# Cross-attention with nested Winograd products: column sums of a softmax taken from inner right sums, and one right sum made by ScalarE and a transfer

## Chip, cores and metric

The kernel runs on one core of a Trainium2 chip. The metric is the device time of one execution in microseconds (us). All data is float32.

## What is computed

Eight independent batches, each with x1 and x2 of 512 channels by 1024 positions. Constants: a projection to 64 channels for queries and keys, and a 512 by 512 matrix for the values.

```python
B, C1, C2, N = (8, 512, 512, 1024)
q = jnp.einsum('bcn,dc->bnd', x1, Wq) + bq
k = jnp.einsum('bcn,dc->bdn', x2, Wk) + bk[:, None]
v = jnp.einsum('bcn,dc->bdn', x2, Wv) + bv[:, None]
attn = jax.nn.softmax(jnp.einsum('bnd,bdm->bnm', q, k), axis=2)
attn_out = jnp.einsum('bcm,bnm->bcn', v, attn)
return attn_out + x1
```

## The kernel before

**Order of the two large products.** The kernel applies the value matrix last: with e the exponentials of the scores, it forms y = x2 · e, divides y by the column sums of e, and multiplies by Wv (`w`). So each batch has two matrix products: y (512 x 1024 times 1024 x 1024) and the output (512 x 512 times 512 x 1024). The scores lie transposed, with the keys m on partitions: in tile `e` of half h (512 queries n each), `e[:, g, i, :]` holds 128 keys by 512 queries, two groups g of four tiles i.

**Products of products.** Each of the two is split in 2 x 2 blocks and computed with Winograd's seven products instead of eight (table `MULT`): the left factors are 11, 12, 22 and the sums S1 to S4 of blocks of the left matrix (`LEFT`), the right ones 11, 21, 22 and the sums T1 to T4 of blocks of the right matrix. They come in the order 1, 2, 6, 7, 5, 3, 4. Many of the seven are split once more in the same way (the inner products). For such an inner product, number i, `left_stream` makes its four left sums on VectorE in four pieces of 256 columns (L522, tile `aI`), and `right_stream` its right sums in three pieces: T1 and T3 together (L537, 1024 columns), T2 (L542, 512), T4 (L544, 512). The tiles are called after the product: eI1 is product 1, eI2 product 2, eI6 product 6, eI7 product 7. Products 1 and 2 of y take right blocks of the exponentials of half 0 themselves, tiles g = 0 and g = 1; products 6, 7, 5 and 4 take outer sums, product 3 the exponentials of half 1. Product 6 is split for batches 2 to 5 only. On TensorE an inner product is a run of matmuls at L555 into the banks `chain` and `third`; ScalarE's copies (L746) carry partial results from `chain` to the banks of the outer product (`ps_ya`, `ps_yc`).

**One period.** `period(s, n, nn, nnn)` does the rest of batch s and the beginning of batch n, the next one: all its products but the first few are for s, and the scores, the softmax and the first sums for n are put between. Every engine's queue is written out by hand: the order of calls in `period` is the order in which each engine runs its instructions, and `weave` takes one operation in turn from several streams. Nothing is reordered at run time; an instruction that waits holds up all that follow on its engine.

**Softmax of half 0 of batch n**, during batch s: the maximum (`highest`), subtraction of it (`lower`, VectorE L322), exponentials in place (`exponential`, ScalarE L331). The column sums are then made as follows:

- `copy_first`: ScalarE copies the first tile of e into `sum` (L971, 1024 columns).
- `add_tile`, three times: a transfer that GpSimd issues adds another tile of e to `sum` (L966, 512 KB each).
- `total`: VectorE adds the two groups (`fold_halves`, L266, 512 columns), GpSimd sums over the partitions (L291, `den`), and a transfer spreads row 0 of it over 128 partitions x 4 columns (`few`).
- `invert`: VectorE's reciprocal of `few` (L299), and a transfer to a row in DRAM; `spread`: a transfer that brings that row to all partitions. `scale_y` (L875) multiplies blocks of y by it.

**End of a period** (L1505 on), where one batch hands over to the next. The output of batch s ends with product 4 (`second(4)`, TensorE L464 into the banks `ps_oc`, with T4 of y as its right factor, tile `yT`), while VectorE makes the sums of products 1 and 2 of batch n. Then come `total(n, 0)` and `evict_o(s, "21")`: VectorE adds to block 21 of the output what two banks `ps_oc` hold (L937, tile `o`, two instructions of 512). In the next period TensorE starts with products 1 and 2 of y; the copies of product 2's chain (L746, `ps_yc`) write into the banks that this eviction empties. Then VectorE makes S2 of product 6 and the others (L522).

**T4 of y** (a right sum of the outer output product) is `sum_y(s, "T4")`, a VectorE subtraction of 1024 columns: y21 − T2 (L429). In batches 1 to 6 it stands in the handover behind the first left sums of product 1 of batch n, ahead of the first right sums (L537, eI1) and the addition to `ps_oc` (L719), which ends output product 7. Before that addition ScalarE copies a part to the same bank (L711).

Of the kernel before, what the change touches and what calls it, by code (L numbers as in the profile page):

```python
# [9 lines left out]
F32 = mybir.dt.float32  # L10
AF = mybir.ActivationFunctionType
ALU = mybir.AluOpType
# [3 lines left out]
def kernel(  # L16
# [47 lines left out]
    nc = tc.nc  # L64
    P = 128
    B, C, N = x1.shape
    D = 64
    CT = C // P
    H = 512
# [5 lines left out]
    sb = ctx.enter_context(tc.tile_pool(name="sb", bufs=1))  # L75
# [188 lines left out]
    def fold_halves(s, h, op):  # L264
        f = s.mx[h]
        nc.vector.tensor_tensor(f[:, 0, :], f[:, 0, :], f[:, 1, :], op)  # L266
# [29 lines left out]

    def invert(s, h):

        nc.vector.reciprocal(s.few[h], s.few[h])  # L299
        s.row[h] = row = dram.tile([1, H], F32, tag="row", name=f"row_{s.b}_{h}")  # L300
        nc.gpsimd.dma_start(row.rearrange("o (p f) -> (o p) f", p=P), s.few[h])

    def spread(s, h):

# [117 lines left out]
    def sum_y(s, k):  # L422
        y = s.y
        if k == "T2":
            for n in ("T1", "T2", "T4"):
                y[n] = sb.tile([P, 2, H], F32, tag=f"y{n}", name=f"y{n}_{s.b}")
            nc.vector.tensor_tensor(y["T2"], y["11"], y["T3"], ALU.add)
        else:
            nc.vector.tensor_tensor(y[k], y["22" if k == "T1" else "21"], y["T2"], ALU.subtract)  # L429

    HALVES = left, right = slice(0, H // 2), slice(H // 2, H)


# [45 lines left out]
    def multiply_o1(s):  # L479
# [34 lines left out]

    def left_stream(s, i, x, tag):

        v = {f"{p + 1}{q + 1}": x[:, ts(q, MH // 2), ts(p, P)] for p in range(2) for q in range(2)}
        sums = sb.tile([P, 4, MH // 2, P], F32, tag=tag, name=f"aI{i}_{s.b}")
        s.inner[i] = v
        for z, (k, x, y, op) in enumerate(LEFT):  # L520
            v[k] = sums[:, z]
            nc.vector.tensor_tensor(v[k], v[x], v[y], op)  # L522
            yield
# [4 lines left out]
    def right_stream(s, i, x, *tags):  # L528

        half = x.shape[1] // 2  # L530
        v = {f"{q + 1}{r + 1}": x[:, ts(q, half), ts(r, H // 2)] for q in range(2) for r in range(2)}
        last = 4 // len(tags)
        shape = [P, last, half, H // 2]
        sums = [sb.tile(shape, F32, tag=t, name=f"eI{i}{t}_{s.b}") for t in tags]
        both, t2, t4 = sums[0][:, 0:2], sums[-1][:, last - 2], sums[-1][:, last - 1]
        part = x.rearrange("p (q k) (r n) -> p q k r n", q=2, r=2)
        nc.vector.tensor_tensor(  # L537
            both, part[:, :, :, 1, :], part[:, 0].rearrange("p k r n -> p r k n"), ALU.subtract
        )
        s.inner[i, "t"] = v | {"T1": both[:, 0], "T3": both[:, 1], "T2": t2, "T4": t4}  # L540
        yield
        nc.vector.tensor_tensor(t2, both[:, 0], v["22"], ALU.subtract)  # L542
        yield
        nc.vector.tensor_tensor(t4, v["21"], t2, ALU.add)  # L544
        yield
# [326 lines left out]
    def scale_y(s, *ks):  # L872
        for k in ks:
            rden = s.rden[k in ("T3", "22")].unsqueeze(1).to_broadcast([P, 2, H])
            nc.vector.tensor_tensor(s.y[k], s.y[k], rden, ALU.mult)  # L875
# [120 lines left out]
    def head_keys(s, n, bank):  # L996
# [3 lines left out]
        def add(*tiles):  # L1000
            for c in tiles:
                for h, r in ((0, lo), (1, hi)):
                    nc.tensor.matmul(
                        ps[r, n], wk_sb[:, c, :], s.x[:, c, HALVES.index(n), h], start=(c == 0), stop=(c == CT - 1)
                    )
# [5 lines left out]
    def head(s):  # L1011
# [101 lines left out]
    def period(s, n, nn, nnn):  # L1113

        late = s.b >= 1
        five = late and n is not None
# [36 lines left out]
                highest(n, 0)  # L1153
            return then

        def add_exponential(i):
            exponential(n, 0, i)
            add_tile(n, 0, i)

        def while_11(j):  # L1160
            if five and j == 0 and nn:
                add_exponential(3)

        def while_57(j):
            if nn:
                exponential(n, 1, j)
            elif j == 0:
                add_exponential(3)
# [7 lines left out]
        def first_sum():  # L1176
            copy_first(n, 0)
            add_tile(n, 0, 1)

        if not s.t:  # L1180
            open_t(s)
# [178 lines left out]
        if n:  # L1360
            if s.b:
                load_a(n, "11")
            if nn is None:
                load_x(n, x1)
            if nn:
                scores_and(n, 1, 2, "a", nothing)
            else:
                scores(n, 1, 0)()
                scores(n, 1, 1)()
                third = scores(n, 1, 2, "a")  # L1370
                third(0)
# [34 lines left out]
        if five:  # L1406
            fold(n, 1, 3, "max", ALU.max)
            products = multiply_41(s)
            next(products)
            highest(n, 1)  # L1410
            next(products, None)
            if s.six:
                exponential(n, 0, 2)
            if nn is None:
                first_sum()
                begin_s1(n)
                end_s1(n)
        elif late:
            weave(multiply_41(s))
        else:  # L1420
            multiply_seeded(s, 4, "r", hooks)()
            begin_s1(n)
            end_s1(n)
# [52 lines left out]
        if n:  # L1476
            if five:
                sums_1 = left_stream(n, 1, n.a["11"], "i2")
                next(sums_1)
                weave(sums_1, singly(lambda: lower(n, 1, 2), lambda: sum_y(s, "T4")))  # L1480
        if n is None:
            inner_right(s, "o3", s.y["22"], "eT2")
            multiply_573(s)
# [35 lines left out]
        if n:  # L1519
            weave(  # L1520
                in_turn(
                    sums_n1 if s.six else right_stream(n, 1, n.e[0][:, 0], "yT1", "yT2"),
                    singly(*([lambda: lower(n, 1, 3)] if s.b == 0 else [])),
                    right_stream(n, 2, n.e[0][:, 1], "eT4"),
                ),
                left_stream(n, 2, n.a["12"], "aI3" if n.b > 1 else "aS4"),
            )
            last = evict_o(s, "12")
            if five:
                negate(n, "S3")  # L1530
# [50 lines left out]
```

## Time and profile before

| | |
|---|---|
| runs, us | 664.44, 665.40, 666.31 (median 665.4) |
| profiled execution: span from first to last instruction | 662.5 us |
| granted clock of TensorE | 1.000 |
| TensorE matmuls (PE) | 657.7 us busy, 99% of the span |
| VectorE (DVE) | 622.4 us, 94% |
| ScalarE (ACT) | 379.7 us, 57% |
| GpSimd (POOL) | 225.5 us, 34% |
| DMA queue q0 (software_dynamic) | 50.4% of 16 DMA engines' span |
| DMA queue q1 (hardware_dynamic) | 30.6% |

The page gives the span of the profiled execution and no other time of it; the runs in the first row are executions of their own, and the difference of their median and the span is 2.9 us.

How to read rows. A row of the groups reads: line, engine, operation, out<-in by the program's names (batch numbers left out), partitions x elements, how many times; behind the bar busy time, mean duration of one in ns, and idle time ahead of it with what ended most of it. In a timeline a row begins with the start in us from the span's start and the duration in us of one instruction or a run of equal ones (x2, x4); in square brackets may stand how long the engine was idle ahead of it and what it waited for. In the waits of an engine stand: engine, line waiting, what was waited for, us in total, times, longest. In a table of windows stand the window, its length, busy time of TensorE and number of its matmuls, then weight loads, VectorE, ScalarE, GpSimd, and at the end granted clock, share of the DMA engines and GB/s; the first two numbers behind the window are its length and TensorE's busy time. On PE a line of the kernel shows its matmuls, on PEld the loads of their weights.

### The profile page before, as it was taken

What the parts mean: (1) busy time and instruction counts of PE and PEld (TensorE: products, weight loads), DVE (VectorE), ACT (ScalarE), POOL (GpSimd) and SP (SyncE); (2) the same over time, 40 slices, a digit from 0 to 9 for tenths busy, and PEclk for the clock granted to TensorE, in tenths of its full rate; (3) what the DMA queues carried; (4) which work ended last, traced back from release to release, by engine and by line L of the source; (5) the groups of instructions that cost most, each with busy time, mean ns of one, the idle gap of its engine ahead of it and who ended that gap; (6) DMA issues with size and microseconds to landing.
All of it is one profiled execution on the core that took longest, in us unless ns stands there. A gap on an engine that the chain in (4) does not pass through costs nothing.

```text
span 662.5 us, 7988 instructions
## 1 busy us (share of the span) xinstructions
PE 657.7 (99%) x2626; PEld 433.7 (65%) x2626; DVE 622.4 (94%) x869; ACT 379.7 (57%) x728; POOL 225.5 (34%) x192
## 2 busy tenths in 40 slices
PE   9999999999999999999999999999999999999997
PEld 4435755756658666677666686576865757666865
DVE  1999999999999998999989999899999989999997
ACT  3755557446475575665756647656576555574332
POOL 0125215631255412463126431364213640244300
PEclk9999999999999999999999999999999999999999
DMA  8688578994899859998599995998948994399604
GB/s 329 259 281 255 118 256 147 210 261 142 276 162 227 240 164 299 194 245 198 166 290 204 227 232 148 276 209 203 273 91 192 216 243 176 77 180 242 132 15 152
DMA packets 51545, 135.88 MB, mean 205 GB/s; under 512 B 5680, under 2 KB 6192, under 8 KB 51504
## 3 DMA queue, kind: packets, MB, share of 16 engines
q0 software_dynamic: 24512, 61.94, 50.4%
q1 hardware_dynamic: 26848, 73.29, 30.6%
q8 instruction: 21, 0.34, 0.2%
q10 hardware_dynamic: 144, 0.14, 0.1%
q14 instruction: 20, 0.16, 0.1%
HBM read 87.83 MB, written 16.81 MB: 158 GB/s over the span
## 4 chain that ended last, share of the span: by engine, by line
PE 98%; DMA 1%; SPq 0%; DVE 0%; issue 0%
PE ps_yc L555 9%; PE ps_ya L555 7%; PE ps_oc L464 7%; PE ps_oa L689 7%; PE ps_s L236 6%; PE ps_ya L464 4%; PE ps_oa L464 4%; PE ps_q L191 4%; PE ps_i5chain L555 3%; PE ps_i4b L840 3%; PE ps_k L191 3%; PE ps_i3chain L555 3%; PE ps_i7chain L555 3%; PE ps_oc L840 3%; PE ps_i1chain L555 3%; PE ps_i2chain L555 3%
## 5 line engine op out<-in xcount | busy, mean ns | idle before, releaser
L331 ACT ACTIVATE e<-e 128x1024 f32<-128x1024 f32 x60 | 63.4, 1059 | 25.6 <-DVE e L322 25.2
L291 POOL PARTITION_ALL_REDUCE den<-sum x16 | 52.8, 3298 | 59.0 <-DVE sum L266 54.2
L322 DVE TENSOR_TENSOR e<-e,top 128x1024 f32<-128x1024 f32 x60 | 72.3, 1217 | 0.2 <-POOL top L272 0.2
L272 POOL PARTITION_ALL_REDUCE top<-max x16 | 31.4, 1960 | 94.1 <-DVE max L266 68.1
L966 POOL DMA_DIRECT2D sum<-e x21 | 25.9, 1235 | 82.0 <-ACT sum L971 32.6
L245 ACT COPY e<-ps_s 128x512 f32<-128x512 f32 x90 | 47.8, 622 | 10.1 <-PE ps_s L236 7.6
L236 PE MATMUL ps_s<-q,k 64*128 64x512 f32 (+1 forms) x188 | 46.6, 598 | 0.0
L256 DVE TENSOR_TENSOR max<-max,e 128x1024 f32<-128x1024 f32 x30 | 36.6, 1218 | 0.3
L236 PEld LDWEIGHTS ps_s<-q,k 64*128 64x128 f32 x188 | 17.5, 186 | 19.9 <-issue 17.4
L875 DVE TENSOR_TENSOR y<-y,den 128x1024 f32<-128x1024 f32 x24 | 29.2, 1220 | 0.3
L522 DVE TENSOR_TENSOR aI<-a,aI 128x256 f32<-128x256 f32 x60 | 28.1, 468 | 0.9
L746 ACT COPY ps_yc<-ps_i7chain 128x256 f32<-128x256 f32 x32 | 11.4, 357 | 30.2 <-PE ps_i7chain L555 26.1
L689 PE MATMUL ps_oa<-yT,w_S 128*128 128x512 f32 x56 | 27.4, 592 | 0.0
L307 POOL DMA_DIRECT2D den<-row x12 | 6.7, 558 | 59.0 <-DMA row<-few 47.8
L522 DVE TENSOR_TENSOR aI<-a 128x256 f32<-128x256 f32 x60 | 26.3, 464 | 0.0
L689 PE MATMUL ps_oa<-y,w_S 128*128 128x512 f32 x56 | 26.3, 592 | 0.0
L191 PE MATMUL ps_q<-x_in_x_dram,wqk_sb 128*64 128x512 f32 x112 | 25.6, 598 | 0.0
L746 ACT COPY ps_ya<-ps_i5chain 128x256 f32<-128x256 f32 x32 | 11.5, 361 | 24.2 <-PE ps_i5chain L555 20.0
L464 PE MATMUL ps_oa<-yT,w_S 128*128 128x512 f32 x56 | 25.2, 593 | 0.0
L464 PE MATMUL ps_oc<-yT,w 128*128 128x512 f32 x56 | 25.2, 592 | 0.0
L555 PE MATMUL ps_yc<-e,aI 128*128 128x256 f32 x92 | 23.6, 379 | 0.0
L746 ACT COPY ps_ya<-ps_i1chain 128x256 f32<-128x256 f32 x28 | 10.0, 357 | 22.1 <-PE ps_i1chain L555 18.5
(346 smaller groups left out, 1840.0 us busy)
## 6 DMA issues: line engine op xcount, KB each, us to landing
x_in_x_dram<-in_x_dram SPq DMA_DIRECT2D x60, 512.0 KB, 7.9
a<-in_x2T_dram SPq DMA_DIRECT2D x32, 512.0 KB, 7.0
aS<-in_x2T_dram POOLq DMA_DIRECT2D x21, 512.0 KB, 10.2
sum<-e POOLq DMA_DIRECT2D x21, 512.0 KB, 6.2
eT<-eT POOLq DMA_DIRECT2D x16, 512.0 KB, 11.9
r<-in_x_dram POOLq DMA_DIRECT2D x14, 512.0 KB, 8.3
uo<-in_x_dram POOLq DMA_DIRECT2D x14, 512.0 KB, 9.8
out_dram<-r SPq DMA_DIRECT2D x14, 512.0 KB, 8.9
```

Of the source, the lines that this page charges most:

```text
L191: nc.tensor.matmul(ps[r, :], w_sb[:, c, :], s.x[:, c, ts(h, H)], start=(c == 0), stop=(c == CT - 1),)
L236: nc.tensor.matmul(ps[g][:, n], s.k[r, ts(i, P)], s.q[r, ts(h, H)][:, n], start=True, stop=True)
L245: nc.scalar.copy(e[:, g, i, :], ps[g])
L256: nc.vector.tensor_tensor(f, e[:, :, 0, :] if i == 1 else f, e[:, :, i, :], op)
L291: nc.gpsimd.partition_all_reduce(s.den[h], s.mx[h][:, 0, :], P, ReduceOp.add)
L322: nc.vector.tensor_tensor(e, e, top, ALU.subtract)
L331: nc.scalar.activation(e, e, AF.Exp)
L464: nc.tensor.matmul(ps, left[ka][:, k, ts(j, P)], right[kb][:, k, :], start=opens and k == 0, stop=i in (2, 3, 4) and k == n_k - 1, skip_gr ...
L522: nc.vector.tensor_tensor(v[k], v[x], v[y], op)
L555: nc.tensor.matmul(ps, s.inner[i][ka][:, k, :], s.inner[i, "t"][kb][:, k, :], start=opens and k == 0, stop=z in (2, 3, 4) and k == n_k - 1 ...
L689: nc.tensor.matmul(ps, w[ka][:, k, ts(j, P)], s.y[kb][:, k, :], start=False, stop=i == 3 and k == 1, skip_group_check=True,)
L840: nc.tensor.matmul(ps, s.inner[i][ka][:, k, :], s.inner[i, "t"][kb][:, k, :], start=opens and k == 0, stop=z in (2, 3, 4) and k == n_k - 1 ...
```

## The change

**Column sums of half 0** for batches 2 to 7 (`total_0`). For inner products 1 and 2, whose right blocks are tiles of e, the inner sums get other signs: the left ones by the table `LEFT_SUM`, and the right ones are T1 = 12 − 11, T3 = 22 + 12, T2 = T1 + 22, T4 = 21 − T2. The products stay equal. With these signs T4 + T3 is 21 + 11 and T3 is 22 + 12: the sums over the two row blocks of that part of e. They are made by four VectorE pieces of 512 columns (L573) instead of three pieces. Left pieces keep their number and size. `total_0` adds the T4/T3 pairs of products 1 and 2 in one VectorE instruction of 1024 columns (L282), whose output order interleaves the two halves of columns in runs of 4; the fold of halves, the sum over partitions and a transfer follow as before, the last to 64 partitions x 8 (`fews`). `invert` adds the two halves of that small tile (64x4, L316) ahead of the reciprocal (64x8). For batches 2 to 7 the copy of the first tile and the three transfers are gone; the exponentials stay where they were. Batch 1 keeps the old way.

**T4 of y** for batches 1 to 5. `copy_yt4`: ScalarE writes −T2 (1024 columns, L450) right behind the last copies of the products 4 and 1 (`multiply_41`). A transfer from GpSimd adds block 21 of y to it (L1463), once that has been scaled. The subtraction on VectorE is gone there; batches 0, 6 and 7 keep it.

```diff
+    def total_0(s):
+        s.mx[0] = f = sb.tile([P, 2, H], F32, tag="fold", name=f"sum_{s.b}_0", bufs=2)
+        x, y = (s.inner[i, "m"].rearrange("q z k (p f) -> q z k p f", p=D) for i in (1, 2))
+        nc.vector.tensor_tensor(f.rearrange("q k (p z f) -> q z k p f", p=D, z=2), x, y, ALU.add)
+        fold_halves(s, 0, ALU.add)
+        s.den[0] = sb.tile([P, H], F32, tag="den", name=f"den_{s.b}_0", bufs=2)
+        nc.gpsimd.partition_all_reduce(s.den[0], f[:, 0, :], P, ReduceOp.add)
+        s.few[0] = sb.tile([D, 2, H // P], F32, tag="fews", name=f"fews_{s.b}", bufs=2)
+        nc.gpsimd.dma_start(
+            s.few[0].rearrange("p z f -> p (z f)"), s.den[0][0:1, :].rearrange("o (p f) -> o p f", p=D)
+        )
...
     def invert(s, h):
-        nc.vector.reciprocal(s.few[h], s.few[h])
+        few = s.few[h]
...
+        if h == 0 and s.b > 1:
+            nc.vector.tensor_tensor(few[:, 0, :], few[:, 0, :], few[:, 1, :], ALU.add)
+            to = row.rearrange("o (z p f) -> (o p) z f", z=2, p=D)
+        nc.vector.reciprocal(few, few)
+        nc.gpsimd.dma_start(to, few)
...
+    def copy_yt4(s):
+        nc.scalar.mul(s.y["T4"], s.y["T2"], -1.0)
...
+    LEFT_SUM = (
+        ("S3", "21", "11", ALU.subtract),
+        ("S1", "21", "22", ALU.subtract),
+        ("S2", "11", "S1", ALU.subtract),
+        ("S4", "12", "S2", ALU.subtract),
+    )
...
+            for k, x, y, op in (
+                ("T1", "12", "11", ALU.subtract),
+                ("T3", "22", "12", ALU.add),
+                ("T2", "T1", "22", ALU.add),
+                ("T4", "21", "T2", ALU.subtract),
+            ):
+                nc.vector.tensor_tensor(v[k], v[x], v[y], op)
+                yield
...
-            elif nn:
-                first_sum()
...
+            if nn:
+                copy_yt4(s)
             if s.six:
                 exponential(n, 0, 2)
             if nn is None:
-                first_sum()
                 begin_s1(n)
                 end_s1(n)
...
         scale_y(s, "21")
+        if five and nn:
+            nc.gpsimd.dma_start(s.y["T4"], s.y["21"], accum_op=ALU.add)
...
-        if s.six:
-            add_tile(n, 0, 2)
-        elif five:
-            add_exponential(2)
+        if five and not s.six:
+            exponential(n, 0, 2)
...
             second(4)
-            total(n, 0)
+            if five:
+                total_0(n)
+            else:
+                total(n, 0)
             evict_o(s, "21")
```

**Where it moves instructions.** VectorE's queue in the handover from batch 2 to batch 3, from behind the sum of outer blocks to the eviction of block 21 of the output. Each row has the line, the operation, the tile written, the tiles read and the shape (names end in the batch and a running number); eI1 and eI2 are right sums of products 1 and 2, aI left sums of product 2, `e_0` the exponentials of half 0. Before:

```order
L542 TENSOR_TENSOR eI1yT_3_1814<-eI1yT_3_1813,e_0_1446 128x512
L522 TENSOR_TENSOR aI_3_1830<-a_3_1734 128x256
L544 TENSOR_TENSOR eI1yT_3_1814<-e_0_1446,eI1yT_3_1814 128x512
L522 TENSOR_TENSOR aI_3_1830<-a_3_1734 128x256
L537 TENSOR_TENSOR eI2eT_3_1834<-e_0_1446 128x1024
L522 TENSOR_TENSOR aI_3_1830<-a_3_1734,aI_3_1830 128x256
L542 TENSOR_TENSOR eI2eT_3_1834<-eI2eT_3_1834,e_0_1446 128x512
L522 TENSOR_TENSOR aI_3_1830<-a_3_1734,aI_3_1830 128x256
L544 TENSOR_TENSOR eI2eT_3_1834<-e_0_1446,eI2eT_3_1834 128x512
L266 TENSOR_TENSOR sum_0_1649<-sum_0_1649 128x512
L937 SCALAR_TENSOR_TENSOR o_2_1854<-ps_oc_2_7_1779,wqk_sb,uo_2_1754 128x512
```

And now (lines of the changed kernel; L550 is the old L522, L978 the old L937):

```order
L573 TENSOR_TENSOR eI1yT_3_1813<-e_0_1449 128x512
L550 TENSOR_TENSOR aI_3_1829<-a_3_1735 128x256
L573 TENSOR_TENSOR eI1yT_3_1812<-eI1yT_3_1812,e_0_1449 128x512
L550 TENSOR_TENSOR aI_3_1829<-a_3_1735 128x256
L573 TENSOR_TENSOR eI1yT_3_1813<-e_0_1449,eI1yT_3_1812 128x512
L550 TENSOR_TENSOR aI_3_1829<-a_3_1735,aI_3_1829 128x256
L573 TENSOR_TENSOR eI2eT_3_1835<-e_0_1449 128x512
L550 TENSOR_TENSOR aI_3_1829<-a_3_1735,aI_3_1829 128x256
L573 TENSOR_TENSOR eI2eT_3_1835<-eI2eT_3_1835,e_0_1449 128x512
L573 TENSOR_TENSOR eI2eT_3_1835<-e_0_1449,eI2eT_3_1835 128x512
L282 TENSOR_TENSOR sum_0_1850<-eI1yT_3_1813,eI2eT_3_1835 128x2x128x4
L266 TENSOR_TENSOR sum_0_1850<-sum_0_1850 128x512
```

Ten rows stood ahead of the eviction (L937), and thirteen stand there now: a row of eI2 that reads the same as its neighbour (the second piece of product 2, behind the fourth aI) is left out above, and the eviction follows behind the last row. Of product 1's pieces T1 alone is made further up; before, T1 and T3 were. The new sum of 1024 columns (L282) stands between the last right sum and the fold, in the place of nothing, and reads that right sum.

GpSimd's queue in the same period (batch 2, the softmax of batch 3), from the sums of exponentials to the loads for the output. Before:

```order
L966 DMA sum_0_1649<-e_0_1446 128x2x512
L169 DMA aS_3_1652<-in_x2T_dram 128x1024
L272 ISA top_1_1725<-max_1_1676 128x512
L966 DMA sum_0_1649<-e_0_1446 128x2x512
L900 DMA uo_2_1754<-in_x_dram 128x2x512
L966 DMA sum_0_1649<-e_0_1446 128x2x512
L942 DMA r_2_1765<-in_x_dram 128x2x512
L181 DMA aS_3_1810<-in_x2T_dram 128x1024
```

And now (L941 is the old L900, L983 the old L942):

```order
L169 DMA aS_3_1652<-in_x2T_dram 128x1024
L272 ISA top_1_1725<-max_1_1676 128x512
L1463 DMA yT_2_1681<-y_2_1741 128x1024
L941 DMA uo_2_1756<-in_x_dram 128x2x512
L983 DMA r_2_1766<-in_x_dram 128x2x512
L181 DMA aS_3_1809<-in_x2T_dram 128x1024
```

The three transfers that summed exponentials are gone, and the one that adds y21 to T4 of y stands where the second of them stood, ahead of the load for output block 21 (`uo`).

More of the change, by code (lines that the diff above doesn't have):

```diff
@@ L297, in invert @@
     def invert(s, h):
-        nc.vector.reciprocal(s.few[h], s.few[h])
+        few = s.few[h]
         s.row[h] = row = dram.tile([1, H], F32, tag="row", name=f"row_{s.b}_{h}")
-        nc.gpsimd.dma_start(row.rearrange("o (p f) -> (o p) f", p=P), s.few[h])
+        to = row.rearrange("o (p f) -> (o p) f", p=P)
+        if h == 0 and s.b > 1:
[3 more added lines that the diff above has]
+        nc.gpsimd.dma_start(to, few)
     def spread(s, h):
@@ L519, in left_stream @@
         s.inner[i] = v
-        for z, (k, x, y, op) in enumerate(LEFT):
+        for z, (k, x, y, op) in enumerate(LEFT_SUM if i in (1, 2) else LEFT):
             v[k] = sums[:, z]
@@ L534, in right_stream @@
         sums = [sb.tile(shape, F32, tag=t, name=f"eI{i}{t}_{s.b}") for t in tags]
+        if i in (1, 2):
+            for z, k in enumerate(("T1", "T2", "T4", "T3")):
+                v[k] = sums[z // last][:, z % last]
+            s.inner[i, "t"], s.inner[i, "m"] = v, sums[-1][:, last - 2 : last]
+            for k, x, y, op in (
[6 more added lines that the diff above has]
+                yield
+            return
         both, t2, t4 = sums[0][:, 0:2], sums[-1][:, last - 2], sums[-1][:, last - 1]
@@ L1154, in scores_0 @@
             return then
-        def add_exponential(i):
-            exponential(n, 0, i)
-            add_tile(n, 0, i)
         def while_11(j):
             if five and j == 0 and nn:
-                add_exponential(3)
+                exponential(n, 0, 3)
         def while_57(j):
@@ L1167, in while_57 @@
             elif j == 0:
-                add_exponential(3)
+                exponential(n, 0, 3)
             else:
@@ L1174, in early_s2 @@
             add_11(n, "S2")
-        def first_sum():
-            copy_first(n, 0)
-            add_tile(n, 0, 1)
         if not s.t:
@@ L1479, in period @@
                 next(sums_1)
-                weave(sums_1, singly(lambda: lower(n, 1, 2), lambda: sum_y(s, "T4")))
+                weave(
+                    sums_1, singly(lambda: lower(n, 1, 2), *([] if nn else [lambda: sum_y(s, "T4")]))
+                )
         if n is None:
```

## Prediction

> **What bounds the kernel now.** I read the page first (busy shares and the chain that ended last), then the waits of PE, then the windows cut by batch, and last the timelines of each engine where one batch hands over to the next.
>
> ```profile
> PE 657.7 (99%) x2626; PEld 433.7 (65%) x2626; DVE 622.4 (94%) x869; ACT 379.7 (57%) x728; POOL 225.5 (34%) x192
> PE 98%; DMA 1%; SPq 0%; DVE 0%; issue 0%
> PE ps_warm L1029 <- DVE warm L1026: 1.0, 1, 1.0
> PE ps_ka L1003 <- DMA x_head<-in_x2h_dram: 0.3, 1, 0.3
> 280.00:360.30 80.30, 80.30 (x329) 55.04 (x329) 76.89 (x109) 49.53 (x96) 30.41 (x26) 1.00 0.90 220
> ```
>
> The chain is 98% PE, and PE waited 1.3 us in all, both times in the head. In the batch from 280.00 to 360.30 PE is busy for 80.30 of 80.30 us at clock 1.00 and DVE for 76.89. So PE's row of matmuls is the time. The change takes no matmul away, so it has nothing to win there: transfers that it removes delay nobody on PE (0.3 us of waits on DMA). What it can do is lose, where DVE, with 3.4 us to spare in 80, comes later than PE needs it. The question is where DVE's new work stands and how much slack is there.
>
> **What DVE gains and where it goes.** For batches 1 to 5 the subtraction that made T4 of y is gone from DVE (L429). In the handover from batch 2 to 3:
>
> ```profile
> 267.38 1.22 DVE L429 TENSOR_TENSOR yT<-y,yT 128x1024 f32<-128x1024 f32 x1
> 268.85 1.22 DVE L537 TENSOR_TENSOR eI1yT<-e 128x1024 f32<-128x1024 f32 x1
> 269.48 0.36 ACT L711 COPY ps_oc<-ps_io7chain 128x256 f32<-128x256 f32 x1
> 269.99 0.69 DVE L719 TENSOR_TENSOR ps_oc<-ps_oc,vo 128x512 f32<-128x512 f32 x1
> ```
>
> Without L429, and with L537 cut to half its size there, DVE would reach L719 1.7 us sooner. But L719 adds to the bank that ACT's copy L711 fills, and that ends at 269.48 + 0.36 = 269.84. DVE waits, and at most 0.15 us of the 1.7 survives; I count it as nothing.
>
> **What is added behind that point.** Rows of DVE from there to the eviction of block 21 of the output (L937, o), which empties the banks ps_oc; first batch 2 to 3, then 1 to 2:
>
> ```profile
> 275.57 0.68 DVE L542 TENSOR_TENSOR eI1yT<-eI1yT,e 128x512 f32<-128x512 f32 x1
> 276.18 0.42 DVE L522 TENSOR_TENSOR aI<-a 128x256 f32<-128x256 f32 x1
> 276.51 0.68 DVE L544 TENSOR_TENSOR eI1yT<-e,eI1yT 128x512 f32<-128x512 f32 x1
> 277.45 1.22 DVE L537 TENSOR_TENSOR eI2eT<-e 128x1024 f32<-128x1024 f32 x1
> 281.06 1.40 DVE L937 SCALAR_TENSOR_TENSOR o<-ps_oc,wqk_sb,uo 128x512 f32<-128x512 f32 x2
> ...
> 195.23 1.22 DVE L537 TENSOR_TENSOR eI1yT<-e 128x1024 f32<-128x1024 f32 x1
> 200.05 0.68 DVE L542 TENSOR_TENSOR eI2eT<-eI2eT,e 128x512 f32<-128x512 f32 x1
> 200.76 0.69 DVE L544 TENSOR_TENSOR eI2eT<-e,eI2eT 128x512 f32<-128x512 f32 x1
> 201.38 0.68 DVE L266 TENSOR_TENSOR sum<-sum 128x512 f32<-128x512 f32 x1
> 201.98 1.40 DVE L937 SCALAR_TENSOR_TENSOR o<-ps_oc,wqk_sb,uo 128x512 f32<-128x512 f32 x2
> ```
>
> From start to start, 512 columns take 0.60 us (201.38 to 201.98), 256 take 0.33 (276.18 to 276.51), 1024 take 1.14 (268.85 to 269.99, above), and an instruction right behind the one whose result it reads starts 0.1 later (200.05 to 200.76 is 0.71). After the change there stand in batch 2 to 3: seven pieces of 512 (T2, T3, T4 of product 1, all four of product 2), four left sums of 256, the new sum of 1024, the fold of halves, and three restarts (T4 behind T2, the sum behind T4, the fold behind the sum): 4.20 + 1.32 + 1.14 + 0.60 + 0.30 = 7.56 us. Before it was 281.06 − 275.57 = 5.49. **DVE is 2.07 us late** at L937. In batch 1 to 2, where no piece is done ahead, it is 8 × 0.60 + 1.32 + 1.14 + 0.60 + 0.30 = 8.16 against 201.98 − 195.23 = 6.75: 1.41 late. Batches 3 to 4 and 4 to 5 repeat the first case. Batch 6 to 7 is like 1 to 2, and keeps its L429 besides.
>
> The new sum is the one operation that no row shows: it writes runs of 4 columns. I take 1.14, as for any 1024, the nearest row, also because L537, which reads its input in runs of 256, takes the same 1.22 as L429, which doesn't. Below, I allow 0.1; above, another 1.14, as if it were two of them. By the Trainium skill's Vector Engine (DVE) Microarchitecture Reference, section "5.2 Measured stream behaviour on trn2 (trn3 not measured)", an output in runs of 2 or 8 adjacent words keeps the full rate; that would leave the sum below as it is, and its opposite is a rival.
>
> **What PE needs, and when.** How PE shows an operand that comes late: here ACT's copy ended at 398.04, the weights started at 398.08 and the matmul at 398.09.
>
> ```profile
> 397.68 0.36 ACT L746 COPY ps_yc<-ps_i3chain 128x256 f32<-128x256 f32 x1 [0.33 <-ACT uy L863]
> 398.08 0.51 PEld L555 LDWEIGHTS ps_i3chain<-eI3eT,aI 128*128 128x128 f32 x3 [0.32 <-ACT ps_yc L746]
> 398.09 0.70 PE L555 MATMUL ps_i3chain<-eI3eT,aI 128*128 128x256 f32 x2
> ...
> 204.00 1.03 PE L555 MATMUL ps_i2chain<-eI2eT,aI 128*128 128x256 f32 x4
> 208.94 0.41 DVE L522 TENSOR_TENSOR aI<-aS,aI 128x256 f32<-128x256 f32 x1
> 210.04 1.03 PE L555 MATMUL ps_i6chain<-eI6y,aI 128*128 128x256 f32 x4
> ...
> 284.35 1.03 PE L555 MATMUL ps_i2chain<-eI2eT,aI 128*128 128x256 f32 x4
> 288.02 0.41 DVE L522 TENSOR_TENSOR aI<-aS,aI 128x256 f32<-128x256 f32 x1
> 290.39 1.03 PE L555 MATMUL ps_i6chain<-eI6y,aI 128*128 128x256 f32 x4
> ```
>
> So an operand may end 0.05 before its matmul and no later. Two places follow L937. (a) The copy of product 2's chain writes the bank that L937's first half empties, and the chain's next matmul waits for that copy. Batch 1 to 2: the copy must start by 204.00 − 0.05 − 0.36 = 203.59; the first half of L937 ends about 201.98 + 0.74 = 202.72, so the slack is about 0.84, and 1.41 late costs PE 0.57. Batch 2 to 3: 284.35 − 0.41 = 283.94 against 281.80: slack 2.11, no cost. (b) S2 of product 6 (L522). Batch 1 to 2: 208.94 + 0.41 = 209.35, needed at 209.99: slack 0.64, cost 0.77 in all ((a) within it). Batch 2 to 3: 288.43, needed at 290.34: slack 1.91, cost 0.16. Batch 5 to 6 has no split product 6; (a) alone is at its limit there and costs nothing.
>
> For batch 6 to 7 DVE stays late up to product 7:
>
> ```profile
> 608.61 0.16 DVE L299 RECIPROCAL few<-few 128x4 f32<-128x4 f32 x1
> 615.62 1.58 DVE L537 TENSOR_TENSOR eI7yT<-e 128x1024 f32<-128x1024 f32 x1
> 618.32 1.03 PE L555 MATMUL ps_i7third<-eI7yT,aI 128*128 128x256 f32 x4
> ```
>
> The added small sum ahead of the reciprocal costs at least the 0.16 of that reciprocal and a restart of 0.1, so DVE is 1.67 late. T3 of product 7 (L537) ends at 617.20 and is needed at 618.27: slack 1.07, cost 0.60. In the other batches the small sum falls behind both places, and the lateness dies at the waits that DVE has anyway later in the batch, such as
>
> ```profile
> 253.95 0.70 DVE L833 TENSOR_TENSOR ps_oc<-ps_oc,v 128x512 f32<-128x512 f32 x1 [0.95 <-ACT ps_oc L849]
> ```
>
> If that cover were too thin, each of five batches would add what is left over, a few tenths.
>
> **The other edits.** On ACT a copy of 1024 (L971) goes and a negation of 1024 comes, ahead of the evictions at 258.34; ACT idles 1.18 there, and the negation takes the 1.06 of L156, so it fits, with 0.1 left. On POOL the transfer that completes T4 of y takes the place of one that summed exponentials; it waits for L875, ahead of the load for output block 21.
>
> ```profile
> 282.22 1.06 ACT L156 ACTIVATE aS<-aS 128x1024 f32<-128x1024 f32 x1
> 258.34 0.58 ACT L475 COPY uo<-ps_oa 128x512 f32<-128x512 f32 x1 [1.18 <-PE ps_oa L464]
> 258.28 1.22 DVE L875 TENSOR_TENSOR y<-y,den 128x1024 f32<-128x1024 f32 x1
> DMA to landing us min/median/max: 4.8/6.2/10.3
> 273.14 3.60 PE L464 MATMUL ps_oc<-yT,w 128*128 128x512 f32 x8
> ```
>
> L875 ends at 259.50; issued at about 259.8, the transfer lands between 264.6 and 270.1 by the summing transfers (4.8 to 10.3 us), and PE wants T4 at 273.1. Spare: 3 us. The load queued behind it on POOL is for the eviction at 281.06, 20 us on. So nothing of this is on the path.
>
> **Sum**: 0.77 + 3 × 0.16 + 0 + 0.60 = 1.85 us. The span goes from 662.5 to 664.4. The page gives a span and no time of its own; the runs' median, 665.4, is 2.9 above the span, and I leave that as it is: **667.3**.
>
> **Rivals.**
> - *DVE's lateness is swallowed: not slower.* If the 0.15 that I dropped and a shorter sum take 0.4 off, the three middle batches cost nothing, batch 1 to 2 costs 0.37 and the last 0.20: 0.6 us, 666.0. It decides at about 1.9 us late in the middle batches. For it: my slacks there are within 0.2 of the lateness. Against it: batch 1 to 2 has only 0.64. Range 665.2 to 666.6. Chance 0.22.
> - *The sum with short runs is slow.* Every 0.1 beyond 1.14 goes straight to PE in six batches, 0.6 us. A quarter more (one lost slot per run of 4; 512 further columns take 0.54 us, so 256 slots take 0.27) makes 1.85 + 6 × 0.27: 668.9; double makes 674.1. Chance 0.15. The Trainium skill, SBUF — State Buffer, section "Door 1: The DMA port swizzle", says that an access that crosses into a new 16-byte line pays a penalty; if a hop to the next line but one pays it, each of the 256 runs does, and the time is the 668.9 above. No row here shows such a write.
> - *T4 lands late.* From 13.3 us after its issue (259.8 to 273.1), each us costs five, one a batch: at 14.0 some 3.5, 670.8. For it: the DMA engines are 0.90 busy in the window quoted. Against: a summing transfer stood at that very place and the queue now holds fewer. Chance 0.07.
>
> **How the numbers follow.** Forecast 0.53, with 666.5 to 668.3; the rivals 0.22, 0.15, 0.07; 0.03 for something that quickens PE, of which I see no sign. The bound of 0.3%, about what a measurement of this kernel can tell from no change, is 2.0 us, and my sum lies just inside it. Slower by more: 0.23 of the forecast and all of the last two rivals, 0.45; within: 0.30 + 0.22 = 0.52; faster: 0.03. The range 665.2 to 669.8 holds the first rival, the forecast and the lower third of the second.
>
> **What would show it.** PE's waits name DVE or ACT (ps_i2chain, ps_i6chain, ps_i7third) where they named only the head; L937 (o) stands about 2 us later against ps_i1chain, and in batch 1 to 2 PE stops for 0.5 to 0.6 ahead of ps_i2chain. The sum of 1024 shows 1.22 or more. An idle of DVE ahead of the addition to ps_oc (L719) shows that removing L429 won nothing. If PE shows no such waits, the slack was misread; if PE waits for a transfer into yT, the third rival holds.

## The result, and the profile after

The changed kernel takes 668.25 us (median of 10 runs, 667.35 to 669.82), the kernel before 665.08 us in 10 runs beside it (664.35 to 667.44). The ratio is 1.0042, with a 95% interval of 1.0029 to 1.0055: slower by 1.9 to 3.7 us. The forecast was 667.3.

The head of the page of the changed kernel:

```profile
span 665.4 us, 7983 instructions
...
PE 659.8 (99%) x2626; PEld 432.7 (65%) x2626; DVE 626.3 (94%) x890; ACT 379.1 (57%) x727; POOL 208.8 (31%) x179
```

The waits of TensorE in it, with us in total, times and the longest:

```profile
PE ps_warm L1070 <- DVE warm L1067: 1.0, 1, 1.0
PE ps_i2chain L596 <- ACT ps_yc L787: 0.5, 1, 0.5
PE ps_i7third L596 <- DVE eI7yT L578: 0.5, 1, 0.5
```

The span grew by 2.9 us, and GpSimd has 16.7 us less to do: the transfers are gone and nobody gained by it. The list of waits names two of the places that the prediction named, 1.0 us in all. The rest is in waits too short for that list. It can be read off, since TensorE runs the same 2626 matmuls in the same order in both kernels: the start of each after the change, minus its start before, steps up wherever TensorE lost time, and stays level elsewhere. Worked out so from the two traces:

| handover | shift behind it, us | lost in it | predicted |
|---|---|---|---|
| (ahead of all) | −0.38 | | |
| 1 to 2 | 0.63 | 1.01 | 0.77 |
| 2 to 3 | 1.07 | 0.44 | 0.16 |
| 3 to 4 | 1.51 | 0.44 | 0.16 |
| 4 to 5 (1.33 ahead of it) | 1.78 | 0.45 | 0.16 |
| 5 to 6 | 2.02 | 0.24 | 0 |
| 6 to 7 | 2.89 | 0.87 | 0.60 |

All of this loss, 3.45 us, is in the six handovers; 0.38 us was won in the head and early in batch 1, and 0.18 at a wait for ScalarE ahead of product 3 in batch 4. Behind batch 1's beginning every step up stands at ps_i2chain, ps_i6chain or product 7, but for one of 0.05 us at product 1 of batch 2, which the first row of the table already holds. No other place in a batch loses more than 0.01 us: the lateness does not go on through the batch, as the prediction had it.

VectorE in the handover from batch 2 to 3, with the rows that answer to those of the prediction (L573 are the right sums, L760 was L719, L978 was L937):

```profile
268.46 0.69 DVE L573 TENSOR_TENSOR eI1yT<-e 128x512 f32<-128x512 f32 x1
270.49 0.70 DVE L760 TENSOR_TENSOR ps_oc<-ps_oc,vo 128x512 f32<-128x512 f32 x1 [1.34 <-ACT ps_oc L752]
...
276.20 0.68 DVE L573 TENSOR_TENSOR eI1yT<-e 128x512 f32<-128x512 f32 x1
...
280.55 0.68 DVE L573 TENSOR_TENSOR eI2eT<-eI2eT,e 128x512 f32<-128x512 f32 x1
281.27 0.69 DVE L573 TENSOR_TENSOR eI2eT<-e,eI2eT 128x512 f32<-128x512 f32 x1
282.00 1.22 DVE L282 TENSOR_TENSOR sum<-eI1yT,eI2eT 128x1024 f32<-128x1024 f32 x1
283.25 0.69 DVE L266 TENSOR_TENSOR sum<-sum 128x512 f32<-128x512 f32 x1
283.86 1.40 DVE L978 SCALAR_TENSOR_TENSOR o<-ps_oc,wqk_sb,uo 128x512 f32<-128x512 f32 x2
```

Without the subtraction for T4 of y, VectorE stands idle for 1.34 us ahead of the addition to ps_oc, waiting for ScalarE: removing that work won nothing. From the first piece (276.20) to the eviction (283.86) it now takes 7.66 us, where it took 5.49.

What follows on ScalarE and TensorE in the same handover:

```profile
284.70 0.36 ACT L787 COPY ps_yc<-ps_i2chain 128x256 f32<-128x256 f32 x1 [0.79 <-DVE o L978]
285.10 0.73 PEld L596 LDWEIGHTS ps_i2chain<-eI2eT,aI 128*128 128x128 f32 x4 [0.37 <-ACT ps_yc L787]
285.11 1.13 PE L596 MATMUL ps_i2chain<-eI2eT,aI 128*128 128x256 f32 x4
```

This is the chain in three rows: ScalarE's copy waits for the eviction, the weights wait for the copy, and the matmul starts with the weights. Its four matmuls take 1.13 us; before the change the same four took 1.03. Before, the weights for them began to load 0.22 us ahead of the first matmul (at 284.35), and not 0.01:

```profile
284.13 0.84 PEld L555 LDWEIGHTS ps_i2chain<-eI2eT,aI 128*128 128x128 f32 x4
```

### The profile page after: what moved, and what is told of

The parts are those of the page before. It is cut to its first block, busy times and chain, and to the rows that moved or that the text cites. A ratio compares the mean times of both kernels' runs of the same rounds, so it can differ in the third digit from the quotient of the medians.

```text
span 665.4 us, 7983 instructions
## 1 busy us (share of the span) xinstructions
PE 659.8 (99%) x2626; PEld 432.7 (65%) x2626; DVE 626.3 (94%) x890; ACT 379.1 (57%) x727; POOL 208.8 (31%) x179
## 4 chain that ended last, share of the span: by engine, by line
PE 87%; DVE 11%; issue 1%; ACT 0%; DVEq 0%; ACTq 0%
PE ps_yc L596 8%; PE ps_ya L596 6%; PE ps_s L236 6%; PE ps_oa L730 6%; PE ps_oc L485 6%; PE ps_q L191 4%; PE ps_oa L485 4%; PE ps_k L191 3%; PE ps_ya L485 3%; PE ps_i7chain L596 3%; PE ps_i5chain L596 3%; PE ps_i4b L881 3%; PE ps_i3chain L596 3%; PE ps_i2chain L596 2%; PE ps_oc L881 2%; PE ps_i4chain L881 2%
## 5 line engine op out<-in xcount | busy, mean ns | idle before, releaser
L550 DVE TENSOR_TENSOR aI<-a,aI 128x256 f32<-128x256 f32 x60 | 28.1, 468 | 1.1
L550 DVE TENSOR_TENSOR aI<-a 128x256 f32<-128x256 f32 x60 | 24.0, 425 | 0.0
L983 POOL DMA_DIRECT2D r<-in_x_dram x14 | 18.3, 1309 | 15.5 <-ACT r L971 15.5
```

## The experiments

The theory after the result: the whole cost is VectorE's lateness in the handovers, met at the bank that the eviction of block 21 empties (ps_i2chain) and at the sums behind it (ps_i6chain, product 7). The rivals: ScalarE's and GpSimd's new work for T4 of y costs; VectorE's total work counts, wherever it stands; each wait has a fixed price.

### Each half alone

T4 of y alone, put into the kernel before:

```diff
+            if nn:
+                copy_yt4(s)
...
+        if five and nn:
+            nc.gpsimd.dma_start(s.y["T4"], s.y["21"], accum_op=ALU.add)
...
-                weave(sums_1, singly(lambda: lower(n, 1, 2), lambda: sum_y(s, "T4")))
+                weave(sums_1, singly(lambda: lower(n, 1, 2), *([] if nn else [lambda: sum_y(s, "T4")])))
```

> The kernel before with only the other way of making T4 of y (ScalarE's negation and a transfer, batches 1 to 5). Theory (the cost of the change is VectorE's lateness behind the right sums of product 2): VectorE loses 1.14 us ahead of the addition to ps_oc and then waits there for ScalarE, so nothing moves: 665.1, within 0.4, and no wait of TensorE beyond the head. Rival (the cost comes from ScalarE's or GpSimd's new work for T4, or T4 lands late): 1 us or more above the kernel before, with a wait of TensorE that names yT or a ScalarE copy. A gain of 1 us or more would mean that VectorE's work counts wherever it stands.

It took 664.94 us (11 runs), ratio to the kernel before 1.0003 (0.9994 to 1.0012). TensorE waits only in the head, and VectorE's row ahead of the old L719 shows where the time freed went:

```profile
270.09 0.70 DVE L722 TENSOR_TENSOR ps_oc<-ps_oc,vo 128x512 f32<-128x512 f32 x1 [0.81 <-ACT ps_oc L714]
```

This half of the change costs nothing and wins nothing. In the changed kernel its transfer lands 5.5 to 5.8 us after its issue, some 7 us before product 4 needs it; GpSimd's row, the times to landing, and TensorE's row of product 4:

```profile
260.72 0.92 POOL L1463 DMA_DIRECT2D yT<-y  x1 [2.90 <-PE ps_oa L485]
...
DMA to landing us min/median/max: 5.5/5.6/5.8
...
273.77 2.74 PE L485 MATMUL ps_oc<-yT,w 128*128 128x512 f32 x6
```

The sums alone, that is, the changed kernel with the same lines taken out:

> The changed kernel with T4 of y made by VectorE as before; only the new sums of half 0 are left of the change. Theory: the subtraction of 1.14 us falls into the 1.34 us that VectorE idles ahead of the addition to ps_oc in the middle handovers, and is 0.3 us too long for the 0.81 us in the handover from batch 1 to 2: the time of the changed kernel, 668.2, to 0.4 above it. Rival (the work for T4 on ScalarE and GpSimd is what costs): 1 us or more below the changed kernel. Rival (VectorE's total work counts): 5 x 1.14 us above it, 673.9.

It took 669.02 us (5 runs), ratio 1.0057 (1.0045 to 1.0070), 0.4 us above the range that was expected. The matmul starts tell why: each handover from 1 to 2 on loses what it loses in the changed kernel, within 0.02 us (1.00, 0.45, 0.45, 0.45, 0.23, 0.87). What its profile has more is 1.15 us at two waits for a load of x at 43 us, in batch 0, where the two kernels are alike, and 0.2 in the handover from 0 to 1. So the subtraction did fit into the idle time, and the cost of the change sits in the sums. From 1 to 2 the expectation had seen 0.3 us left over; there VectorE idled 0.20 us more, for TensorE ahead of the next eviction (L978), and that took it up. VectorE's rows of the changed kernel there:

```profile
189.09 0.70 DVE L760 TENSOR_TENSOR ps_oc<-ps_oc,vo 128x512 f32<-128x512 f32 x1 [0.81 <-ACT ps_oc L752]
190.00 1.41 DVE L978 SCALAR_TENSOR_TENSOR uo<-ps_oc,wqk_sb,uo 128x512 f32<-128x512 f32 x2 [0.20 <-PE ps_oc L596]
```

### The same work in another place

One piece more ahead of the addition to ps_oc (and the order T1, T2, T3, T4):

```diff
             for k, x, y, op in (
                 ("T1", "12", "11", ALU.subtract),
-                ("T3", "22", "12", ALU.add),
                 ("T2", "T1", "22", ALU.add),
+                ("T3", "22", "12", ALU.add),
...
                 next(sums_n1)
+                next(sums_n1)
```

> The changed kernel with one piece more of product 1's right sums (T2, right behind T1) ahead of the addition to ps_oc, for batches 2 to 5 as s (handovers 2 to 3 up to 5 to 6); VectorE's work is the same and only stands elsewhere. Theory: VectorE idled 1.34 us there, so the eviction of block 21 comes 0.72 us earlier, 1.45 instead of 2.17 late against a slack of 2.04: the waits at ps_i2chain and ps_i6chain go in these handovers (3 x 0.44 + 0.23 = 1.55 us), those of 1 to 2 and 6 to 7 stay: 666.7. Rival (VectorE's total work or the DMA queues set the time): 668.2, unchanged.

It took 666.51 us (6 runs), ratio 1.0026 (1.0014 to 1.0037), near the 666.7 of the theory. In its trace VectorE's idle time ahead of the addition is 0.55 instead of 1.34, and from 2 to 3 up to 5 to 6 the matmul starts show no step at all. VectorE's row there:

```profile
271.65 0.70 DVE L760 TENSOR_TENSOR ps_oc<-ps_oc,vo 128x512 f32<-128x512 f32 x1 [0.55 <-ACT ps_oc L752]
```

What is left is the 0.87 us from 6 to 7, and a cost of the edit itself: where no piece is done ahead, T3 now comes behind T2, and the matmul that needs it loses 0.40 from 0 to 1, and 0.91 from 1 to 2, where 0.12 of the old waits stays besides. The theory had no such cost, so that the whole time came out so near is partly chance; the level starts in the middle handovers are what bears it out. TensorE's waits name 1 to 2 and 6 to 7:

```profile
PE ps_i1third L596 <- DVE eI1yT L573: 0.7, 1, 0.7
PE ps_i7third L596 <- DVE eI7yT L578: 0.5, 1, 0.5
```

VectorE does as much work as in the changed kernel, so it is not the work that costs, but where it stands.

The eviction of block 21 ahead of the new sum:

```diff
             if five:
-                total_0(n)
+                evict_o(s, "21")
+                total_0(n)
             else:
                 total(n, 0)
-            evict_o(s, "21")
+                evict_o(s, "21")
```

> The changed kernel with the eviction of block 21 ahead of the new sum and the fold. Theory with two places in the handover (the bank that the eviction empties, for product 2, and S2 of product 6 behind it): the first is relieved, but S2 comes as late as it did, and TensorE waits there for the whole lateness (0.4 in the middle handovers, 1.0 from 1 to 2); only the handover 5 to 6, with no split product 6, gains its 0.23: 668.0. Rival (the bank alone is what costs): the waits at ps_i2chain go and nothing comes in their place, 0.79 + 3 x 0.24 + 0.23 = 1.7 us less: 666.5.

It took 675.21 us (5 runs), ratio 1.0171 (1.0156 to 1.0187): 7 us more than the theory allowed, and neither it nor the rival had a kernel slower than the changed one. The waits at ps_i2chain are gone, but a new one came, for T1 and T3 of product 6:

```profile
PE ps_i6third L596 <- DVE eI6yT L578: 4.1, 4, 1.4
```

VectorE from 2 to 3 in this kernel:

```profile
283.48 1.40 DVE L978 SCALAR_TENSOR_TENSOR o<-ps_oc,wqk_sb,uo 128x512 f32<-128x512 f32 x2
284.80 1.21 DVE L282 TENSOR_TENSOR sum<-eI1yT,eI2eT 128x1024 f32<-128x1024 f32 x1
286.04 0.69 DVE L266 TENSOR_TENSOR sum<-sum 128x512 f32<-128x512 f32 x1
286.65 0.69 DVE L804 TENSOR_TENSOR ps_ya<-ps_ya,v 128x512 f32<-128x512 f32 x1
287.25 4.03 DVE L358 TENSOR_TENSOR eT<-eT,e 128x1024 f32<-128x1024 f32 x2
```

And GpSimd's sum over the partitions there:

```profile
286.84 3.23 POOL L285 PARTITION_ALL_REDUCE den<-sum  x1 [4.97 <-DVE sum L266]
```

The two outer sums L358 take 4.03 us. In the changed kernel a pair of the same shape takes 2.43 where GpSimd sums nothing, and 2.71 at this place:

```profile
273.85 2.43 DVE L358 TENSOR_TENSOR eT<-e,e 128x1024 f32<-128x1024 f32 x2
...
285.78 2.71 DVE L358 TENSOR_TENSOR eT<-eT,e 128x1024 f32<-128x1024 f32 x2
```

GpSimd's sum in the changed kernel:

```profile
284.05 3.23 POOL L285 PARTITION_ALL_REDUCE den<-sum  x1 [3.78 <-DVE sum L266]
```

If a pair's own work is 2.43, it began at 287.25 + 4.03 − 2.43 = 288.85 with the eviction first, and at 286.06 in the changed kernel: each time 2.01 us after GpSimd's sum over the partitions had started (286.84 and 284.05). So here a VectorE sum with all its operands in SBUF is held up until 2.0 us behind that start. Instructions that read PSUM are not: in the changed kernel the eviction takes its 1.40 and L804 its 0.69 under the same GpSimd instruction. That is what the theory had left out: with the fold ahead of the eviction, the hold-up lies under the eviction and L804, and 0.28 us of it shows; with the eviction first it lies under L804 alone, and 1.60 shows: a middle handover loses 1.65 us instead of 0.44. By the matmul starts, the other three handovers lose 2.2, 1.1 and 2.2 instead of 1.01, 0.24 and 0.87; together that is the 7 us. In the two last, which have no split product 6, the outer sums are late in the same way (a pair takes 4.03 and 4.04 us), and TensorE loses its time at later places of the batch. The Trainium skill, SBUF — State Buffer, section "SBUF: two separate sides", says that VectorE and GpSimd share a pair of ports as an exclusive lock, held for the whole instruction, against which a VectorE operation with two SBUF inputs blocks. The traces agree on who is blocked; the hold-up measured is 2.0 us of an instruction that the profile shows with 3.23.

### More and less of the suspected work

The new sum twice:

```diff
         nc.vector.tensor_tensor(f.rearrange("q k (p z f) -> q z k p f", p=D, z=2), x, y, ALU.add)
+        nc.vector.tensor_tensor(f.rearrange("q k (p z f) -> q z k p f", p=D, z=2), x, y, ALU.add)
```

> The changed kernel with the new sum of 1024 columns done twice, one behind the other. Theory: what VectorE is late beyond the slack goes to TensorE us for us, in all six handovers: 6 x 1.25 = 7.5 us above the changed kernel, 675.7, some tenths less where two waits become one. Rival (each wait is a fixed price of restarting, whatever the lateness): within 1.5 us of the changed kernel.

It took 676.06 us (4 runs), ratio 1.0169 (1.0155 to 1.0182): 7.8 us above the changed kernel's median where the theory had 7.5 for 6 x 1.25. The second sum takes 1.26 from start to start, like the first:

```profile
284.18 1.23 DVE L282 TENSOR_TENSOR sum<-eI1yT,eI2eT 128x1024 f32<-128x1024 f32 x1
285.44 1.23 DVE L283 TENSOR_TENSOR sum<-eI1yT,eI2eT 128x1024 f32<-128x1024 f32 x1
```

The wait at ps_i2chain is now there in all six handovers:

```profile
PE ps_i2chain L597 <- ACT ps_yc L788: 7.3, 6, 1.8
```

By the matmul starts each of the six handovers loses 1.25 to 1.28 us more than in the changed kernel. Beyond the slack, lateness goes to TensorE us for us; a fixed price for each wait can't be the whole of it.

Half of the new sum:

```diff
-        x, y = (s.inner[i, "m"].rearrange("q z k (p f) -> q z k p f", p=D) for i in (1, 2))
-        nc.vector.tensor_tensor(f.rearrange("q k (p z f) -> q z k p f", p=D, z=2), x, y, ALU.add)
-        fold_halves(s, 0, ALU.add)
+        x = s.inner[1, "m"]
+        nc.vector.tensor_tensor(f[:, 0, :].rearrange("q (z n) -> q z n", z=2), x[:, :, 0, :], x[:, :, 1, :], ALU.add)
```

> The changed kernel with the new sum of 1024 columns and the fold replaced by one sum of 512 over product 1's pieces alone (it leaves out product 2's part of the column sums and the order of the columns); all else, the four pieces and the work for T4 too, is as in the changed kernel. Theory (VectorE's lateness in the handover): 1.25 us less of it, 0.9 us in the middle handovers, 0.3 from 1 to 2, 0.4 from 6 to 7, all within the slack: 664.9, within 0.5 of the kernel before, and TensorE shows no wait at the handovers. Rival (the four pieces, the small sum or ScalarE's negation cost by themselves): at least 1 us above the kernel before.

It took 665.11 us (11 runs), ratio 0.9999 (0.9990 to 1.0008), and TensorE waits only in the head. This kernel leaves out part of the column sums, so it serves for its time alone. The four pieces, the small sum, ScalarE's negation and the transfers cost nothing as long as VectorE is those 1.25 us earlier.

No fold on VectorE; this tests the hold-up found above:

```diff
-        fold_halves(s, 0, ALU.add)
...
-        nc.gpsimd.partition_all_reduce(s.den[0], f[:, 0, :], P, ReduceOp.add)
+        nc.gpsimd.partition_all_reduce(f, f, P, ReduceOp.add)
...
+            nc.vector.tensor_tensor(few[:, 0], few[:, 0], few[:, 1], ALU.add)
```

> The changed kernel without the fold of halves: GpSimd sums 1024 columns over the partitions instead of 512, and VectorE adds the halves of the small tile. VectorE has 0.72 us less ahead of the eviction of block 21. The traces so far show that a VectorE sum with all operands in SBUF, started while GpSimd's sum over partitions runs, does not end before 2.10 us from that one's start plus its own time (1.21 becomes 2.90 in the kernel with the eviction first). If that hold-up grows with the columns (4.2 us for 1024), the outer sums behind the eviction come 1.35 us later than in the changed kernel, and S2 of product 6 with them: about 6 us above the changed kernel, 674 to 675. Rival (the hold-up is 2.1 us whatever the columns): 0.72 less lateness is worth 2.6 us: 665.6.

It took 678.58 us (4 runs), ratio 1.0201 (1.0186 to 1.0217): slower with less VectorE work, as the hold-up that grows has it, and 4 us worse than its figure. The pair of outer sums on VectorE from 2 to 3:

```profile
289.04 5.08 DVE L360 TENSOR_TENSOR eT<-eT,e 128x1024 f32<-128x1024 f32 x2
```

GpSimd's sum ahead of it:

```profile
287.38 6.11 POOL L283 PARTITION_ALL_REDUCE sum<-sum  x1 [3.13 <-DVE sum L282]
```

The pair began at 289.04 + 5.08 − 2.43 = 291.69, 4.31 us after GpSimd's start, against 2.01 for half the columns. The size was missed because I moved only S2 of product 6: T1 and T3 of it are late as well, each middle handover loses about 2.1 us, 5 to 6 loses 1.8, 6 to 7 2.8 and 1 to 2 4.3. From 1 to 2 the granted clock fell besides (third number from the end, in windows of 2 us), which is 1.7 of the 4.3; the like waits later in the same profile have no such dip, and why this one has is open. The run with this profile was the longest of the four, 679.55 us at a mean clock of 0.997; the others took 677.40 to 678.84 at 0.999 to 1.000:

```profile
214.00:216.00 2.00, 2.00 (x6) 1.55 (x6) 1.97 (x3) 1.11 (x2) 0.35 (x1) 0.50 1.16 209
```

### Repair

Two pieces ahead in batches 1 to 5, where VectorE idles (with the order T1, T2, T3, T4 there alone), and the old sums for batch 7 alone:

```diff
+            if i == 1 and 1 < s.b < B - 1:
+                ops[1:3] = ops[2], ops[1]
...
-            if s.six:
+            if nn:
                 sums_n1 = right_stream(n, 1, n.e[0][:, 0], "yT2", "yT1")
                 next(sums_n1)
+                next(sums_n1)
...
-            if five:
+            if five and nn:
                 total_0(n)
...
             if nn is None:
+                copy_first(n, 0)
+                add_tile(n, 0, 1)
...
```

> The changed kernel with two pieces of product 1's right sums (T1, T2) ahead of the addition to ps_oc for batches 1 to 5, where VectorE idles 0.81 to 1.34 us, and with the old sums (a copy and three transfers) for batch 7 alone. Theory: no handover has lateness beyond its slack, TensorE waits only in the head: 664.9, the time of the kernel before within 0.5, and no less than that, since TensorE's work is the same. Rival (the change costs by the work it adds, wherever that stands): 2 us or more above the kernel before.

It took 664.94 us (11 runs), ratio 1.0006 (0.9995 to 1.0016). TensorE waits only in the head:

```profile
PE ps_warm L1073 <- DVE warm L1070: 1.0, 1, 1.0
PE ps_kc L1047 <- DMA x_head<-in_x2h_dram: 0.5, 1, 0.5
```

Of the 18 summing transfers that the change took away 15 stay away (the five for T4 of y come instead), and the time is that of the kernel before. It doesn't beat it: with TensorE's work unchanged and no wait but these in the head, there was nothing else to win.

## Why the prediction was right, and where its sizes were off

- **The time.** The forecast was 667.3, with 666.5 to 668.3 as its own range, and 668.25 lies at the upper edge of that. The path was right, the sum was too small, and luck made the time look nearer than the sum was: in the traces 0.56 us was won in places that the prediction doesn't have (0.38 in the head and in batch 1, 0.18 in batch 4), and the kernel before took 665.08 where the forecast starts from 665.4. The upper part of the whole range, up to 669.8, was there for a slow new sum, which did not come. Of its two main outcomes the one with the smaller chance came, by a little: it gave 0.45 to a loss of more than 0.3% and 0.52 to less, and 0.42% was measured, with 0.29 to 0.55% as the interval.
- **No gain is possible.** Right: T4 of y alone, half of the new sum and the repair all end at the time of the kernel before, though two of them work with fewer transfers and the first takes 1.14 us of VectorE's work away in five batches.
- **Removing L429 wins nothing.** Right: VectorE idles 1.34 us (0.81 from 1 to 2) at L760 instead, and without the other half of the change the time stays as it was.
- **DVE is 2.07 us late at the eviction.** 2.17 measured (7.66 − 5.49). Most of the tenth is in the restarts: 0.11 to 0.13 us behind a result that the next instruction reads, where I took 0.10. The 1.41 from 1 to 2 and from 6 to 7 came out 0.1 higher in the same way. The new sum took its 1.22 us, as taken; runs of 4 columns in the output cost nothing, so the rival of slow short runs falls. What the prediction cited of the Trainium skill's Vector Engine (DVE) Microarchitecture Reference, section "5.2 Measured stream behaviour on trn2 (trn3 not measured)", that such runs (there of 2 or 8 words) keep the full rate, is borne out by these six rows of 1.22 with runs of 4; the other rule that it cited would have given 668.9 by a slower sum, and no row shows one.
- **What PE needs, and when.** Here the sizes failed: 1.85 predicted, 3.45 measured in the same six places. I counted the hand-overs as free or as 0.05. ScalarE's copy starts 0.10 after the first half of the eviction has ended (283.86 + 0.74 to 284.70). S2 of product 6 ends at 290.83 + 0.41 = 291.24 and its matmul starts at 291.38, 0.14 later; the 0.05 held for ScalarE's copy alone. VectorE's row, and TensorE's:

```profile
290.83 0.41 DVE L550 TENSOR_TENSOR aI<-aS,aI 128x256 f32<-128x256 f32 x1
```

```profile
291.38 1.10 PE L596 MATMUL ps_i6chain<-eI6y,aI 128*128 128x256 f32 x4
```

  These tenths and the one of the line above make 0.6 us of the 1.6 missing. The other 1.0 is a term that I left out: behind each wait the following matmuls start another 0.07 to 0.11 late (four take 1.13 or 1.10 instead of 1.03), and there are 11 such places, two of them in product 7. The rows of ps_i2chain suggest why, but no run tests it: the weights, which otherwise load 0.22 us ahead, load with the first matmul, and the second waits for its own. The term is why ps_i2chain from 2 to 3, with a slack of 283.94 − 281.80 − 0.10 = 2.04 and a lateness of 2.17, lost 0.24 and not 0.13, and why 5 to 6, "at its limit", lost as much. Two of the prediction's slacks are 0.03 off by its own figures (203.59 − 202.72 is 0.87 and not 0.84, 283.94 − 281.80 is 2.14 and not 2.11); the sum hangs on neither.
- **Swallowed lateness.** The rival falls: the slack of 2.1 in the middle handovers was smaller by the hand-over of 0.10, not larger.
- **T4 lands late.** It falls: 5.5 to 5.8 us to landing, where the prediction took 4.8 to 10.3, and no cost in the kernel with this half alone.
- **The small sum** costs 0.18 us from start to start in batch 6 to 7, less than the 0.26 taken; product 7's T3 was 1.69 late (619.33 − 615.62, less the shift of 2.02) and lost 0.63 before what follows a wait, against 0.60. In the other batches it shows 0.64: it stands in the hold-up of GpSimd's second sum, where a left sum stood before. VectorE's rows in batch 6 to 7:

```profile
612.14 0.14 DVE L316 TENSOR_TENSOR fews<-fews 64x4 f32<-64x4 f32 x1
612.32 0.20 DVE L318 RECIPROCAL fews<-fews 64x8 f32<-64x8 f32 x1
...
619.33 1.59 DVE L578 TENSOR_TENSOR eI7yT<-e 128x1024 f32<-128x1024 f32 x1
```

## What to carry to other kernels

Where one engine is busy all the time and waits for no transfer, moving work from transfers to the other engines wins nothing and can cost: look for the place where the engine that takes the work has its least slack before the next consumer, and price it there. Compare the starts of the unchanged instructions of the bounding engine before and after; the steps show every loss, also those that are too short for a list of waits. An idle time that a change opens is worth something only if the work that it adds is moved into it, and a margin of less than a few tenths of a us is no margin, since each hand-over took 0.05 to 0.14 here and each wait was followed by about another tenth.

## What the runs showed of the hardware

- In the handovers a VectorE sum with all operands in SBUF is held up for 2.0 us from the start of GpSimd's sum over partitions of 512 columns (shown with 3.23 us), and for 4.3 us with 1024 (6.11), while VectorE instructions with a PSUM operand run at their usual 0.69 to 0.74. An order that puts PSUM work under GpSimd's instruction hides it. Where VectorE was in such a sum itself when GpSimd's began (batch 1 of the changed kernel, at 138.62), GpSimd's shows 4.13 us and the hold-up ends 3.0 behind its start, so 2.0 is not a constant.
- A wait of TensorE cost a further 0.07 to 0.11 us on the matmul behind the one that waited, at all 11 places.
- A VectorE output in runs of 4 columns ran at the full rate: 1.22 us for 1024 columns, six times.
